# Pair products of both heads in one matmul of 128 rows, on queries copied apart by ScalarE

## The chip, the core and the metric

The kernel runs on one of the eight cores of a Trainium2 chip. A core has five engines with queues of their own: TensorE (PE in the profile; PEld is its weight loads), VectorE (DVE), ScalarE (ACT), GpSimd (POOL) and SyncE (SP), which here issues DMAs. Matrix products go from SBUF, the working memory, to PSUM, eight banks of accumulators. The metric is device time in microseconds (us) of one execution, smaller is better.

## The reference

Two layers of an RWKV block with adaptive layer norms around them, then a feed-forward part with 4-bit quantised operands; 2 batches, 4096 rows, 256 channels, four heads of 64 channels. What the change touches is the recurrence of each head:

```python
def step(state, inp):
    rt, kt, vt, wt = inp
    kv = kt[..., :, None] * vt[..., None, :]
    out = jnp.einsum('bhk,bhkv->bhv', rt, state + u[None, :, :, None] * kv)
    return (state * wt[..., None] + kv, out)
```

The output at row t is the query r_t against the state before it, plus a bonus u for the row's own key and value. The state decays by w, channel by channel, at every row.

## The kernel before

Each batch and layer is walked in 16 blocks of 256 rows: 64 blocks in all. In a block, channels lie on the 128 partitions, in two channel blocks j (two heads each: partitions 0 to 63 and 64 to 127), and the 256 rows are two chunks c of 128. `wkv` (L845) turns the recurrence into matrix products. Within a chunk the weight of the pair (query row t, key row s) is a product of decays between s and t; it is formed level by level. At level l rows are grouped in runs of 2^(l+1); the second half of a run holds queries, the first half keys, and each level multiplies the running products of decay into queries and keys (a DVE product, `pair_view`, L811 and L899) for the level above. `rk` holds queries and keys of a block; `rk2` is a second copy, so that a level can be read while the next is made. Where the copy changes, ACT carries over the half that does not change (L898). Level 0 takes rows in pairs, with the bonus u multiplied in by ACT (`with_bonus`, L818).

`products(l)` (L868) makes the pair products of level l on PE, into the PSUM tile `pa` (two banks). For levels 0 to 4 it goes over two chunks, two channel blocks, four groups q of 32 rows, and the two heads p: 32 matmuls of 64 rows (one head's channels) by 32 columns (the keys of the group), with 32 queries at level 0 and the 16 that are queries at levels 1 to 4 (`queries`, L828). Head p writes bank p. Level 5 has 16 such matmuls, level 6 has 8 of 64 by 64. The products are issued as 0 and 1, 2 and 3, 4 and 5, and 6, each time before the DVE product that overwrites what they read (L887 to L900). DVE then writes each level's pairs through a mask into `diag` (levels 0 to 4, L916), ACT copies levels 5 and 6 and then `diag` into the full 128 by 128 weights `attn` (L919, L928), and `attn` goes against the values v on PE (L961). `kv` are the products of keys and values for the state S.

The order of all work is made by a list planner while the program is built (`Plan`, L118). Nine generators (two batches by two layers, the feed-forward, its two chunks of the last blocks, its weights, the modulation) yield work; each engine's instructions are put out in the order in which the planner expects them to be able to start, from a table of costs (`weight`, L422) and of latencies. Matmuls that follow each other in one generator's step are one piece of work and are not parted. A change of the matmul's shape (rows, columns) counts as a turn of the array. `head_lock` (L696) lets one block at a time into `wkv`, from its bonus to its last product with v. Working tiles come from a stock of 37 slots; a generator goes on only while enough are free (L348). Every recorded instruction has line L294, where the planner gives it out, so tiles' names tell the groups apart.

Of the kernel before, what the change touches and what calls it, by code (L numbers as in the profile page):

```python
# [10 lines left out]
F32 = mybir.dt.float32  # L11
# [7 lines left out]
P = 128  # L19
D = 256  # L20
J = D // P
TT = 256
# [13 lines left out]
SOON = 40.0  # L36
BACK = 104.0
TURNS = 30.0
SLOTS = 37
STAGGER = (12, 60)  # L40
PLANS, JITTER = 1, 8.0
SLOTS2 = 3
# [379 lines left out]
def weight(eng, fn, out, ins):  # L422


    def psum(v):
        return isinstance(v, Later) or v.name.startswith(("pa", "kv"))

    n = max(v.free_size() for v in [out] + ins)
    if eng == "tensor":
        n, rows, cols = out.free_size(), ins[0].shape[0], out.shape[0]  # L430
        if fn == "transpose":
            return 110.0, False
        if rows == P and cols == P:
            return max(4 * n / 2.4 + 6, 195.0 if n == 64 else 265.0 if n == P else 0.0), False
        if n <= 64:
            return {(64, 32): 18.0, (64, 64): 65.0, (P, 64): 65.0}.get((rows, cols), 2 * n), False
        return 0.57 * (4 * n / 2.4 + 6), False
    if eng == "sync":
        return 100.0, False
    wide = [v for v in ins if v.free_size() > 1]  # L440
    if eng == "scalar":
        return 180.0 + n / 1.2 + (85.0 if len(wide) < len(ins) else 0.0), False
    if eng == "gpsimd":
        if out.free_size() <= 8:
            return 360.0 + 170.0 * n, False
        return 90.0 + 2.1 * n, True
    two = sum(not psum(v) for v in wide) >= 2
    if fn in ("tensor_scalar", "tensor_copy"):
        two = not any(psum(v) for v in wide)
        if out.dtype == I32:  # L450
            return 145.0 + n / 1.92, two
    if fn in ("bn_stats", "bn_aggr", "tensor_reduce", "reciprocal"):
        two = False
    if fn == "reciprocal":
        return 150.0 + 6.2 * n, False
    return (205.0 if fn == "scalar_tensor_tensor" and n <= 256 else 150.0) + n / 0.96, two
# [3 lines left out]
def rwkv_adaln_fp4_kernel(ctx: ExitStack, tc: tile.TileContext, a: dict, out: bass.AP):  # L460
# [210 lines left out]
            for m in range(2):  # L671
                nc.gpsimd.memset(carry[i][b][m], 0.0)
    rk2 = keep.tile([P, 2 * J * TT], F32, name="rk2")
    diag = keep.tile([P, 2, C, J, 32], F32, name="diag")
    attn = keep.tile([P, 2, C, J, P], F32, name="attn")
    nc.gpsimd.memset(diag, 0.0)
    nc.vector.memset(kv, 0.0)
    nc.gpsimd.memset(attn, 0.0)
# [136 lines left out]
            v.tensor, v.offset, [v.ap[0], [J * TT - h if changed else J * TT + h, 2], [2 * h, n], [1, h]]  # L815
        )

    def with_bonus(dst, src, odd, u):  # L818

        dv = dst.rearrange("p c j (t two) -> p c j t two", two=2)  # L820
        sv = src.rearrange("p c j (t two) -> p c j t two", two=2)
        pl.scalar.copy(dv[:, :, :, :, 1 - odd], sv[:, :, :, :, 1 - odd])
        for j in range(J):
            pl.scalar.activation(
                dv[:, :, j, :, odd], sv[:, :, j, :, odd], AF.Copy, scale=u[:, j : j + 1]
            )

    def queries(v, l):  # L828
# [7 lines left out]
        t = t[(slice(None),) * len(v.shape) + (1, slice(None))]  # L836
        return t[(slice(None),) * (len(v.shape) - 1) + (0, slice(None))] if l == NLEV - 1 else t

    def level_cols(l):

        wide = [C * J * (64 if m == 6 else 16 if 0 < m < NLEV else 32) for m in range(7)]
        at = sum(wide[0 if l < 4 else 4 : l])
        return slice(at, at + wide[l])

    def wkv(i, b, rk_s, dec_s, v_s):  # L845

# [5 lines left out]
        pl.cur.late = late - RUSH  # L852


        r0, k0 = parts(rk2)
        r, k = parts(rk)
        with_bonus(r0, r, 0, lay[i]["time_first"])
        with_bonus(k0, k, 1, lay[i]["time_first"])
        yield


# [5 lines left out]

        def products(l):  # L868
            R, K = parts(place[l])
            wid = 64 if l == 6 else 32  # L870
            pv = pa[:, :, level_cols(l)].rearrange("p a (c j t) -> p a c j t", c=C, j=J)

            if l < NLEV:
                at0 = [(q, q) for q in (0, 32, 64, 96)]
            else:
                at0 = [(0, 32), (64, 96)] if l == 5 else [(0, 64)]
            for c in range(C):
                for j in range(J):
                    for s0, t0 in at0:
                        for p in range(2):  # L880
                            hp = slice(p * HS, (p + 1) * HS)
                            mm(
                                pv[s0 : s0 + wid, p, c, j, :], K[hp, c, j, s0 : s0 + wid],
                                queries(R[hp, c, j, t0 : t0 + wid], l), True, True,
                            )

        for l in range(7):  # L887
            h = 1 << l
            for m in {1: (0, 1), 3: (2, 3), 5: (4, 5), 6: (6,)}.get(l, ()):
                products(m)  # L890

            n = C * J * P // (2 * h)
            tv = tot.rearrange("p (n two) -> p n two", two=2)
            here, there = place[l] if l else rk, place[l + 1]
            if here is not there:
                pl.scalar.copy(pair_view(there, h, n, False), pair_view(here, h, n, False))  # L898
            pl.vector.tensor_tensor(  # L899
                pair_view(there, h, n), pair_view(here, h, n), tv.rearrange("p n m -> p m n").unsqueeze(3).to_broadcast([P, 2, n, h]), ALU.mult  # L900
            )
            nt = tots_s[:, at : at + n]
            at += n
            pl.vector.tensor_tensor(nt, tv[:, :, 0], tv[:, :, 1], ALU.mult)
            tot = nt

            ready = {3: range(0, 4), 6: range(4, 7)}.get(l, ())
            for m in ready:
                mw = 64 if m == 6 else 32
                mc = level_cols(m)  # L910
                if m < NLEV:
                    dst = queries(diag.rearrange("p a c j t -> p (a c j) t"), m)
                    src = pa[:, :, mc]
                    mask = masks[:, m, : src.shape[2] // (C * J)]
                    mask = mask.unsqueeze(1).unsqueeze(1).to_broadcast([P, 2, C * J, mask.shape[1]])
                    pl.vector.copy_predicated(dst, mask, src)  # L916
                else:
                    for s0, t0 in [(0, 32), (64, 96)] if m == 5 else [(0, 64)]:
                        pl.scalar.copy(  # L919
                            attn[s0 : s0 + mw].rearrange("p a c j t -> p a (c j) t")[:, :, :, t0 : t0 + mw],  # L920
                            pa[s0 : s0 + mw, :, mc].rearrange("p a (n t) -> p a n t", t=mw),
                        )
            yield
        give(dec_s)
# [2 lines left out]
        for q in range(4):  # L927
            qs = slice(32 * q, 32 * (q + 1))  # L928
            pl.scalar.copy(
                attn[qs].rearrange("p a c j t -> p (a c j) t")[:, :, qs],  # L930
                diag[qs].rearrange("p a c j t -> p (a c j) t"),
            )
        bk, pt = pl.bank()
        for c in range(C):
# [21 lines left out]
        for c in range(C):  # L956
            for j in range(J):
                mm(po[:, c, j * P : (j + 1) * P], r[:, c, j, :], S[:, j, :], True, False)
                for p in range(2):
                    hd = slice((2 * j + p) * HS, (2 * j + p + 1) * HS)  # L960
                    mm(po[:, c, hd], attn[:, p, c, j, :], v[:, c, hd], False, p == 1)  # L961
            for j in range(J):
                pl.vector.scalar_tensor_tensor(
                    S[:, j, :], S[:, j, :], tot[:, c, j : j + 1], kv[:, c, j, :], ALU.mult, ALU.add
# [508 lines left out]
```

## Time and profile before

| | |
|---|---|
| median of 3 runs | 3093.93 us (3090.12 to 3097.47) |
| profiled execution: its own time, from first to last instruction (span) | 3081.1 us |
| median less the span | 12.8 us |
| PE busy | 2920.0 us (95%) |
| PEld, weight loads | 2388.7 us (78%) |
| DVE busy | 2345.6 us (76%) |
| ACT busy | 1667.6 us (54%) |
| POOL busy | 1015.7 us (33%) |
| PE records of the pair products (`pa`) | 23552, 278.8 us |
| granted PE clock, mean | 0.981 |

No other time of the profiled execution is given than its span. An fp32 matmul shows as two records on PE and two weight loads. A record's duration holds the way through the array, and records overlap; the pace of a run of equal records is its length less one duration, over the records less one. Idle time in a group's row stands with what ended it. The notation 64*32 in a row is the part of the array that a matmul uses, rows by columns; several such parts work at once where their rows or columns differ. In the last 110 us only the feed-forward of the last blocks is left.

### The profile page before, as it was taken

Reading aid. Unit: us, or ns where it says so; the run is one execution under the profiler, and the core shown is the slowest. Engines: PE = TensorE matmul, PEld = TensorE weight load, DVE = VectorE, ACT = ScalarE, POOL = GpSimd, SP = SyncE. Lnnn points to the kernel's source line nnn. Section 1 sums busy time; section 2 is a strip of 40 time slices with the busy share of each in tenths; the row PEclk is TensorE's granted clock in tenths of the full one; section 3 lists DMA queues with packets and bytes.
Section 4 is the critical chain, followed back from the end, with each engine's and each line's share of the span. In section 5 each row is a group of like instructions: output and inputs, shape, how many; then the busy total and the mean of one; then the engine's idle time right before and its main releaser. Section 6 shows DMA issues by size and latency. Waiting matters only on the chain. (4 is left out here: it accounts for less than half of the span.)

```text
span 3081.1 us, 89987 instructions
## 1 busy us (share of the span) xinstructions
PE 2920.0 (95%) x38460; PEld 2388.7 (78%) x38460; DVE 2345.6 (76%) x6146; ACT 1667.6 (54%) x3478; POOL 1015.7 (33%) x1208
## 2 busy tenths in 40 slices
PE   6899999999999999999999999999999989999997
PEld 4678788777788887888778787787878778787775
DVE  6687876877787877878587777777778776777777
ACT  3465655564565656555564645646456454645452
POOL 2343333333333342333334233242323323232320
PEclk8899999999999999999999999999999999999999
DMA  4000000000000000000000000000000000000000
GB/s 141 12 19 9 15 7 16 3 16 7 13 12 4 20 3 13 11 8 15 5 18 4 10 13 4 19 5 19 4 8 15 3 20 3 6 11 9 9 14 11
DMA packets 35728, 42.56 MB, mean 14 GB/s; under 512 B 2816, under 2 KB 33536, under 8 KB 35328
## 3 DMA queue, kind: packets, MB, share of 16 engines
q1 hardware_dynamic: 35328, 36.81, 3.7%
q8 instruction: 302, 4.95, 0.6%
q14 instruction: 98, 0.80, 0.1%
HBM read 28.41 MB, written 8.39 MB: 12 GB/s over the span
## 5 line engine op out<-in xcount | busy, mean ns | idle before, releaser
L294 POOL TENSOR_TENSOR slot<-slot,slot 128x256 f32<-128x256 f32 (+1 forms) x768 | 578.1, 780 | 819.1 <-DVE slot L294 615.2
L294 ACT ACTIVATE slot<-bank 128x512 f32<-128x512 f32 (+2 forms) x644 | 334.3, 521 | 594.5 <-PE bank L294 563.4
L294 POOL TENSOR_TENSOR tiny<-tiny,nhalf 128x2 f32<-128x2 f32 (+1 forms) x288 | 296.9, 1034 | 874.6 <-DVE tiny L294 852.3
L294 PE MATMUL bank<-slot,cWk 128*128 128x256 f32 x1536 | 364.3, 385 | 4.5 <-DVE slot L294 4.5
L294 PE MATMUL bank<-slot,small 32*128 32x256 f32 (+3 forms) x2816 | 354.9, 359 | 10.3 <-DVE slot L294 6.9
L294 PE MATMUL bank<-cWv,slot 128*128 128x256 f32 x1536 | 342.4, 379 | 0.0
L294 PEld LDWEIGHTS bank<-slot,cWk 128*128 128x128 f32 x1536 | 288.1, 192 | 50.4 <-DVE slot L294 6.5
L294 ACT ACTIVATE slot<-bank,small 128x256 f32<-128x256 f32 (+1 forms) x640 | 250.9, 453 | 138.8 <-PE bank L294 128.7
L294 PEld LDWEIGHTS bank<-cWv,slot 128*128 128x128 f32 x1536 | 290.5, 190 | 39.7 <-issue 0.3
L294 PEld LDWEIGHTS bank<-slot,small 32*128 32x128 f32 (+3 forms) x2816 | 248.5, 178 | 86.2 <-issue 33.9
L294 DVE TENSOR_TENSOR slot<-slot,bank 128x512 f32<-128x512 f32 x192 | 130.7, 681 | 227.2 <-PE bank L294 193.5
L294 DVE TENSOR_TENSOR slot<-slot,slot 128x512 f32<-128x512 f32 x320 | 229.2, 718 | 82.2 <-PE pa L294 46.1
L294 DVE SCALAR_TENSOR_TENSOR slot<-bank,small,slot 128x256 f32<-128x256 f32 x640 | 265.1, 474 | 16.3 <-PE bank L294 16.0
L294 POOL TENSOR_TENSOR slot<-slot 128x512 f32<-128x512 f32 x128 | 140.3, 1098 | 358.4 <-ACT slot L294 253.5
L294 PEld LDWEIGHTS pa<-slot 64*32 64x32 f32 x11264 | 143.5, 109 | 79.9 <-DVE diag L294 35.2
L294 PE MATMUL pa<-slot 64*32 64x16 f32 x11264 | 171.6, 193 | 33.9 <-DVE diag L294 18.8
L294 PE MATMUL bank<-ident,slot 128*128 128x128 f32 x1152 | 176.1, 280 | 22.3 <-DVE slot L294 14.1
L294 DVE SCALAR_TENSOR_TENSOR slot<-slot,small,slot 128x256 f32<-128x256 f32 x384 | 183.4, 516 | 14.9 <-POOL slot L294 14.8
L294 ACT ACTIVATE slot<-slot 128x512 f32<-128x512 f32 x288 | 182.4, 636 | 21.9 <-DVE slot L294 17.3
L294 ACT ACTIVATE slot<-slot,tiny 128x256 f32<-128x256 f32 x256 | 141.6, 596 | 93.3 <-DVE tiny L294 89.9
L294 PE MATMUL bank<-wd,long 128*128 128x256 f32 x768 | 183.0, 389 | 2.2 <-ACT long L294 2.2
L294 PEld LDWEIGHTS bank<-ident,slot 128*128 128x128 f32 x1152 | 136.0, 143 | 57.8 <-DVE slot L294 19.6
(110 smaller groups left out, 5718.7 us busy)
## 6 DMA issues: line engine op xcount, KB each, us to landing
slot<-in_L_attn_x_dram SPq DMA_DIRECT2D x64, 256.0 KB, 2.8
out_dram<-slot SPq DMA_DIRECT2D x64, 128.0 KB, 1.7
slot<-in_L_wmod_dram SPq DMA_DIRECT2D x6, 256.0 KB, 7.7
cWk<-in_L_attn_cWk_dram SPq DMA_DIRECT2D x2, 768.0 KB, 8.1
cWv<-in_L_attn_cWv_dram SPq DMA_DIRECT2D x2, 768.0 KB, 9.4
small<-in_small_dram SPq DMA_DIRECT2D x2, 718.0 KB, 8.4
long<-in_L_ffn_w_down_dram SPq DMA_DIRECT2D x2, 352.0 KB, 2.8
long<-in_L_ffn_w_gate_dram SPq DMA_DIRECT2D x5, 128.0 KB, 2.2
```

Of the source, the lines that this page charges most:

```text
L294: fn(*[real(v) for v in a], **{n: real(v) for n, v in k.items()})
```

## The change

For levels 0 to 4 both heads of a channel block go through one matmul of 128 rows: the keys of 32 rows, all 128 channels, are the weights, and the moving side has two planes, one for each head. In plane p the other head's 64 partitions are zero, so that plane p gives head p's products. The planes lie in three new tiles `own` (level 0; odd levels; even levels), cleared once at the start by POOL; 2048 elements a partition together. Queries are written into the planes by ACT: at level 0 by the bonus, which is issued for each head on its 64 partitions, and at levels 1 to 4 by `apart`, two copies of 64 partitions and 256 elements, issued after the DVE product that makes the level. Levels 0 to 4 then have 16 matmuls each, of 128 rows by 32 columns, with 64 (level 0) or 32 (levels 1 to 4) moving columns. Levels 5 and 6 stay as they are.

The layouts of `diag`, `attn` and `pa` follow: the head is now inside chunk and channel block, and levels 0 to 4 lie each in one bank. The stock has 34 slots for 37. The planner's table has a cost for the new shape.

```diff
@@ -36,7 +36,7 @@
 SOON = 40.0
 BACK = 104.0
 TURNS = 30.0
-SLOTS = 37
+SLOTS = 34
 STAGGER = (12, 60)
 PLANS, JITTER = 1, 8.0
 SLOTS2 = 3
@@ -433,7 +433,7 @@
         if rows == P and cols == P:
             return max(4 * n / 2.4 + 6, 195.0 if n == 64 else 265.0 if n == P else 0.0), False
         if n <= 64:
-            return {(64, 32): 18.0, (64, 64): 65.0, (P, 64): 65.0}.get((rows, cols), 2 * n), False
+            return {(64, 32): 18.0, (P, 32): 17.0 if n <= 32 else 29.0, (64, 64): 65.0, (P, 64): 65.0}.get((rows, cols), 2 * n), False
         return 0.57 * (4 * n / 2.4 + 6), False
     if eng == "sync":
         return 100.0, False
@@ -671,8 +671,11 @@
             for m in range(2):
                 nc.gpsimd.memset(carry[i][b][m], 0.0)
     rk2 = keep.tile([P, 2 * J * TT], F32, name="rk2")
-    diag = keep.tile([P, 2, C, J, 32], F32, name="diag")
-    attn = keep.tile([P, 2, C, J, P], F32, name="attn")
+    diag = keep.tile([P, C, J, 2, 32], F32, name="diag")
+    attn = keep.tile([P, C, J, 2, P], F32, name="attn")
+    own = [keep.tile([P, 2 * J * TT // (1 if m == 0 else 2)], F32, name=f"own{m}") for m in range(3)]
+    for t in own:
+        nc.gpsimd.memset(t, 0.0)
     nc.gpsimd.memset(diag, 0.0)
     nc.vector.memset(kv, 0.0)
     nc.gpsimd.memset(attn, 0.0)
@@ -815,14 +818,16 @@
             v.tensor, v.offset, [v.ap[0], [J * TT - h if changed else J * TT + h, 2], [2 * h, n], [1, h]]
         )
 
-    def with_bonus(dst, src, odd, u):
-
-        dv = dst.rearrange("p c j (t two) -> p c j t two", two=2)
-        sv = src.rearrange("p c j (t two) -> p c j t two", two=2)
-        pl.scalar.copy(dv[:, :, :, :, 1 - odd], sv[:, :, :, :, 1 - odd])
+    def with_bonus(dst, src, odd, u, rows=slice(0, P)):
+
+        dv, sv = (
+            v.rearrange("p c j q (t two) -> p c j q t two", two=2)[rows] for v in (dst, src)
+        )
+        one = "p c j q t -> p (c j q) t"
+        pl.scalar.copy(dv[..., 1 - odd].rearrange(one), sv[..., 1 - odd].rearrange(one))
         for j in range(J):
             pl.scalar.activation(
-                dv[:, :, j, :, odd], sv[:, :, j, :, odd], AF.Copy, scale=u[:, j : j + 1]
+                dv[:, :, j, :, :, odd], sv[:, :, j, :, :, odd], AF.Copy, scale=u[rows, j : j + 1]
             )
 
     def queries(v, l):
@@ -836,11 +841,25 @@
         t = t[(slice(None),) * len(v.shape) + (1, slice(None))]
         return t[(slice(None),) * (len(v.shape) - 1) + (0, slice(None))] if l == NLEV - 1 else t
 
-    def level_cols(l):
-
-        wide = [C * J * (64 if m == 6 else 16 if 0 < m < NLEV else 32) for m in range(7)]
-        at = sum(wide[0 if l < 4 else 4 : l])
-        return slice(at, at + wide[l])
+    def by_head(l):
+
+        return own[0 if l == 0 else 2 - l % 2].rearrange("p (c j q a t) -> p c j q a t", c=C, j=J, q=4, a=2)
+
+    def apart(l, src):
+
+        h = 1 << l
+        sv = src.rearrange("p c j (q n two t) -> p (c j q) n two t", q=4, two=2, t=h)
+        dv = by_head(l).rearrange("p c j q a (n t) -> p (c j q) a n t", t=h)
+        for p in range(2):
+            hp = slice(p * HS, (p + 1) * HS)
+            pl.scalar.copy(dv[hp, :, p], sv[hp, :, :, 1])
+
+    def level_at(l):
+
+        at = {0: (0, 0), 1: (0, 256), 2: (1, 0), 3: (1, 128), 4: (1, 256), 5: (0, 384), 6: (0, 0)}[l]
+        if l < NLEV:
+            return pa[:, at[0], at[1] : at[1] + C * J * (64 if l == 0 else 32)]
+        return pa[:, :, at[1] : at[1] + C * J * (32 if l == 5 else 64)]
 
     def wkv(i, b, rk_s, dec_s, v_s):
 
@@ -852,10 +871,15 @@
         pl.cur.late = late - RUSH
 
 
-        r0, k0 = parts(rk2)
+        _, k0 = parts(rk2)
         r, k = parts(rk)
-        with_bonus(r0, r, 0, lay[i]["time_first"])
-        with_bonus(k0, k, 1, lay[i]["time_first"])
+        by_q = "p c j (q t) -> p c j q t"
+        for p in range(2):
+            with_bonus(
+                by_head(0)[:, :, :, :, p, :], r.rearrange(by_q, q=4), 0, lay[i]["time_first"],
+                slice(p * HS, (p + 1) * HS),
+            )
+        with_bonus(k0.rearrange(by_q, q=4), k.rearrange(by_q, q=4), 1, lay[i]["time_first"])
         yield
 
 
@@ -867,13 +891,20 @@
 
         def products(l):
             R, K = parts(place[l])
-            wid = 64 if l == 6 else 32
-            pv = pa[:, :, level_cols(l)].rearrange("p a (c j t) -> p a c j t", c=C, j=J)
-
+            pv = level_at(l)
             if l < NLEV:
-                at0 = [(q, q) for q in (0, 32, 64, 96)]
-            else:
-                at0 = [(0, 32), (64, 96)] if l == 5 else [(0, 64)]
+                pv = pv.rearrange("p (c j t) -> p c j t", c=C, j=J)
+                for c in range(C):
+                    for j in range(J):
+                        for q in range(4):
+                            qs = slice(32 * q, 32 * (q + 1))
+                            mm(
+                                pv[qs, c, j, :], K[:, c, j, qs],
+                                by_head(l)[:, c, j, q].rearrange("p a t -> p (a t)"), True, True,
+                            )
+                return
+            pv = pv.rearrange("p a (c j t) -> p a c j t", c=C, j=J)
+            wid, at0 = (32, [(0, 32), (64, 96)]) if l == 5 else (64, [(0, 64)])
             for c in range(C):
                 for j in range(J):
                     for s0, t0 in at0:
@@ -881,7 +912,7 @@
                             hp = slice(p * HS, (p + 1) * HS)
                             mm(
                                 pv[s0 : s0 + wid, p, c, j, :], K[hp, c, j, s0 : s0 + wid],
-                                queries(R[hp, c, j, t0 : t0 + wid], l), True, True,
+                                R[hp, c, j, t0 : t0 + wid], True, True,
                             )
 
         for l in range(7):
@@ -903,22 +934,23 @@
             at += n
             pl.vector.tensor_tensor(nt, tv[:, :, 0], tv[:, :, 1], ALU.mult)
             tot = nt
+            if l + 1 < NLEV:
+                apart(l + 1, next(parts(there)))
 
             ready = {3: range(0, 4), 6: range(4, 7)}.get(l, ())
             for m in ready:
                 mw = 64 if m == 6 else 32
-                mc = level_cols(m)
+                src = level_at(m)
                 if m < NLEV:
-                    dst = queries(diag.rearrange("p a c j t -> p (a c j) t"), m)
-                    src = pa[:, :, mc]
-                    mask = masks[:, m, : src.shape[2] // (C * J)]
-                    mask = mask.unsqueeze(1).unsqueeze(1).to_broadcast([P, 2, C * J, mask.shape[1]])
+                    dst = queries(diag.rearrange("p c j a t -> p (c j a) t"), m)
+                    mask = masks[:, m, : 32 if m == 0 else 16]
+                    mask = mask.unsqueeze(1).to_broadcast([P, 2 * C * J, mask.shape[1]])
                     pl.vector.copy_predicated(dst, mask, src)
                 else:
                     for s0, t0 in [(0, 32), (64, 96)] if m == 5 else [(0, 64)]:
                         pl.scalar.copy(
-                            attn[s0 : s0 + mw].rearrange("p a c j t -> p a (c j) t")[:, :, :, t0 : t0 + mw],
-                            pa[s0 : s0 + mw, :, mc].rearrange("p a (n t) -> p a n t", t=mw),
+                            attn[s0 : s0 + mw].rearrange("p c j a t -> p a (c j) t")[:, :, :, t0 : t0 + mw],
+                            src[s0 : s0 + mw].rearrange("p a (n t) -> p a n t", t=mw),
                         )
             yield
         give(dec_s)
@@ -927,8 +959,8 @@
         for q in range(4):
             qs = slice(32 * q, 32 * (q + 1))
             pl.scalar.copy(
-                attn[qs].rearrange("p a c j t -> p (a c j) t")[:, :, qs],
-                diag[qs].rearrange("p a c j t -> p (a c j) t"),
+                attn[qs].rearrange("p c j a t -> p (c j a) t")[:, :, qs],
+                diag[qs].rearrange("p c j a t -> p (c j a) t"),
             )
         bk, pt = pl.bank()
         for c in range(C):
@@ -958,7 +990,7 @@
                 mm(po[:, c, j * P : (j + 1) * P], r[:, c, j, :], S[:, j, :], True, False)
                 for p in range(2):
                     hd = slice((2 * j + p) * HS, (2 * j + p + 1) * HS)
-                    mm(po[:, c, hd], attn[:, p, c, j, :], v[:, c, hd], False, p == 1)
+                    mm(po[:, c, hd], attn[:, c, j, p, :], v[:, c, hd], False, p == 1)
             for j in range(J):
                 pl.vector.scalar_tensor_tensor(
                     S[:, j, :], S[:, j, :], tot[:, c, j : j + 1], kv[:, c, j, :], ALU.mult, ALU.add
```

## The prediction

> **What bounds the kernel now.** I read the page's totals first, then the table of 500 us stretches, then the shapes on TensorE, then what TensorE waits for, and last a timeline of a few blocks for the pace of single matmuls.
>
> ```profile
> span 3081.1 us, 89987 instructions
> ...
> PE 2920.0 (95%) x38460; PEld 2388.7 (78%) x38460; DVE 2345.6 (76%) x6146; ACT 1667.6 (54%) x3478; POOL 1015.7 (33%) x1208
> ```
>
> TensorE (PE) is the only engine near its span. The stretches show that this is not an average over unlike stages:
>
> ```profile
> 0.00:100.00 100.00, 65.54 (x986) 44.65 (x986) 68.76 (x200) 36.58 (x82) 25.26 (x52) 0.88 0.34 114
> 100.00:500.00 400.00, 381.14 (x5245) 315.34 (x5244) 301.60 (x837) 232.49 (x486) 147.15 (x174) 0.97 0.04 12
> 1000.00:1500.00 500.00, 493.61 (x6398) 407.17 (x6396) 387.27 (x1024) 285.99 (x596) 171.40 (x199) 1.00 0.04 11
> 1500.00:2000.00 500.00, 479.09 (x6864) 394.71 (x6852) 380.40 (x1011) 284.11 (x591) 175.21 (x202) 0.98 0.04 11
> 2970.00:3081.10 111.10, 92.82 (x393) 71.26 (x391) 86.42 (x186) 34.49 (x65) 16.81 (x19) 0.95 0.04 12
> ```
>
> The columns after the length are busy us of PE, weight loads, DVE, ACT, POOL, then the granted clock. From 100 to 2850 us PE idles 99.8 of 2750 us in all, so a microsecond of PE work taken out there is nearly a microsecond of time, if the rest keeps up. What PE waits for in that stretch:
>
> ```profile
> PE bank L294 <- DVE slot L294: 19.4, 26, 2.0
> PE pa L294 <- DVE diag L294: 18.5, 24, 1.9
> PE bank L294 <- ACT slot L294: 15.2, 18, 2.4
> ...
> PE kv L294 <- ACT slot L294: 6.9, 12, 1.4
> ...
> PE pa L294 <- ACT attn L294: 3.9, 6, 1.5
> ...
> PE pa L294 <- ACT rk L294: 3.5, 6, 0.9
> ```
>
> ScalarE (ACT) ends only 30.5 us of it (these four ACT lines and 1.0 us for another). The shapes that the change touches, of the pair products (pa) and of the bonus copies:
>
> ```profile
> L294 PE MATMUL pa<-rk 64*32 64x16 f32 x8192 | 96.5, 188 | 8.4 <-DVE diag L294 5.3 <-issue 2.7
> L294 PE MATMUL pa<-slot 64*32 64x16 f32 x8192 | 95.8, 188 | 21.9 <-DVE diag L294 9.4 <-DVE slot L294 6.4 <-DVE tiny L294 4.2
> L294 ACT ACTIVATE rk<-slot,small 128x128 f32<-128x128 f32 x256 | 99.3, 415 | 11.6 <-DVE slot L294 10.6
> L294 ACT COPY rk<-slot 128x256 f32<-128x256 f32 x128 | 54.9, 431 | 0.8
> L294 ACT COPY attn<-diag 32x256 f32<-32x256 f32 x256 | 102.8, 402 | 13.3 <-DVE diag L294 10.3
> ```
>
> Each matmul of this fp32 kernel is two records here. The timeline has the pace (start, length of the run, records):
>
> ```profile
> 1504.45 0.66 PE L294 MATMUL bank<-slot,small 128*64 128x128 f32 x8
> 1505.04 0.73 PE L294 MATMUL pa<-slot 64*32 64x16 f32 x64
> ...
> 1513.01 0.68 PE L294 MATMUL pa<-slot 64*64 64x64 f32 x16 [0.56 <-DVE diag L294]
> 1513.62 0.71 PE L294 MATMUL bank<-slot,small 64*128 64x128 f32 x8
> ...
> 1544.38 0.46 PE L294 MATMUL pa<-slot 64*32 64x32 f32 x32
> ...
> 1556.84 0.69 PE L294 MATMUL kv<-slot,slot 128*64 128x64 f32 x16
> ```
>
> A run's length less one record's mean duration, over the records less one, is the pace. The 64x16 products: (0.73-0.188)/63 = 8.6 ns. Level 5 (N 32, four array tiles at once: two row halves, two column groups; mean 196 ns in its group): (0.46-0.196)/31 = 8.5. Level 6 (64*64, two tiles, N 64, mean 227): (0.68-0.227)/15 = 30.2. kv (128*64, two tiles, N 64, mean 232): (0.69-0.232)/15 = 30.5. The decay projection (128*64, two tiles, N 128, mean 287): (0.66-0.287)/7 = 53.3.
>
> **The change, part by part.** There are 64 blocks (16 row blocks, 2 batches, 2 layers).
>
> Pair products, removed: five levels of 32 matmuls, 320 records x 8.6 = 2.75 us a block. N of 16 or 32 makes no difference to that pace, and neither does having four or eight tiles: it is a floor per record.
>
> Pair products, added: five levels of 16 matmuls, 160 records. Levels 1 to 4 have N 32 on four column tiles. Nearest row: level 5, with the same N, weight columns and number of tiles; only the rows are 128 for 64, and 64*64 against 128*64 (30.2 and 30.5, two tiles each) says that rows alone cost nothing. Low end 8.5, high end half of kv's pace for half its columns, 15.3; I take 8.6, level 5's side. Level 0 has N 64 on four tiles: low end 53.3 x 64/128 x 2/4 = 13.3, high end kv's 30.5 for twice the tiles, 15.3; I take 15. Sum 128 x 8.6 + 32 x 15 = 1.58 us. Saved: 1.17 us a block, 75 us in all (79 at the low ends; 304 ns a block, 19.5 us, if all 160 records go at 15.3).
>
> [...]
>
> Tile shapes: in the built order of instructions the shape changes 968 times before and 1019 times after (mostly 128*32 to 64*32 between levels 4 and 5). One change: level 6's 16 records at 30.2 are 0.48 us, but the next shape starts 0.61 us after (1513.01 to 1513.62), so 0.13 us. +6.5 us; bounds 0 and 6.5.
>
> ACT: the query bonus becomes six instructions on 64 partitions instead of three on 128, and levels 1 to 4 get two copies each. The built program has 576 more copies and 128 more activations, 9 and 2 a block. A 64-partition copy of 256 elements lies between the 402 of 32 partitions and the 431 of 128, so 0.42: 9 x 0.42 + 2 x 0.415 = 4.6 us a block, 295 us. Two more table loads (1283 ns each) are 2.6. ACT goes to 1965 us, 64%: it lies beside PE, but the copies stand before the products. Each copy pair waits for DVE's product of the level before; behind it on ACT's queue wait bank evacuations and the attn copies; PE's products wait for it, and DVE's in-place product of the next level waits for both. Levels 0 and 1, 2 and 3, 4 and 5 stand back to back on PE as before. The cover is other streams' matmuls: between group 0/1 and group 2/3 the built order has, at the paces above, 3.6 us of other PE work (2.7 before), between 2/3 and 4/5 3.0 (3.1), before level 6 1.5 (1.9). Two pairs of copies are 2 x 0.84, inside that. Cost bounds: 0, and all three groups of all blocks waiting a whole pair, 64 x 3 x 0.84 = 161 us. I take the side of the cover, and let ACT's own 30.5 us grow as queues do, by busy/(1-busy): 0.54 gives 1.17, 0.64 gives 1.78, x1.5: +15 us.
>
> Where there is no cover: the first block (PE 65.5 of the first 100 us) and the last two, which the chain of waits runs through from 2926 to 2960 us. Bonus 1.25 us longer and two pairs, 1.7: 3 x 3 = +9 us; bounds 0 and 9.
>
> DVE: the masked copies move as many elements as before; 0, between -2 and +2 us (their 111 us by 2%). POOL clears three tiles once, 2048 elements a partition; diag's 256 took 316 ns, so about 2.5 us under the 34 us that PE idles in the first 100; 0. No DMA is added or moved past another. SBUF: three slots fewer (34 for 37). The least stock for taking on work is unchanged and the cover counted above has not shrunk; I take 0, with an upper bound of the idle growing as 37/34, 9% of 99.8, 9 us.
>
> Sum: -75 + 6.5 + 15 + 9 = -44.5 us on the profiled execution's 3081.1 us span, or 3036.6. The span lies 12.8 us under the median of the runs, 3093.93; I carry that over: **3049.4 us**.
>
> **Rivals.**
> - *The wait takes the place* (slower). ACT serves the copies late, behind evacuations, and the three product groups of each block stand. For it: PE already waits 40 us for inputs of pa in the middle, and the kernel holds one block in this section at a time. Against it: the counted cover, and ACT 36% idle. At the full price: -75 + 6.5 + 9 + 161, 3195 us. It decides from an average of 0.31 us more waiting a group ((75 - 6.5 - 9)/192).
> - *128-row weight loads set the pace.* All records at 15.3: -19.5 + 6.5 + 15 + 9 = +11, 3105 us. For it: kv's pace, the only one with all rows and few columns. Against: 64*64 has the same.
> - *The saving turns to idle time.* The recurrence and DVE's 76% set the time, PE only fills. For it: 4.2% idle from 1500 to 2000 with five streams at work. Against: 1.3% idle from 1000 to 1500, where DVE is as busy. 3094 us, give or take 6.
>
> That the change does not do what it says is out: the built program has 5120 fewer matmuls.
>
> **How the numbers follow.** Forecast 0.77, wait 0.11, pace 0.07, idle 0.05. The likeliest case's own range: all low ends without a stall, -79, 3015; up to 40 us of stalls in place of 15 and ten more for the clock (granted at 0.97 to 1.00 between 100 and 2000 us above), 3085. To leave out no more than 2 in 10 I take 3015 to 3100: under it and beyond it about one in ten each. Under 0.2% (6 us) the measurement can't tell from no change. Faster 0.80 (the forecast and the mild ends of the rivals), same 0.05, slower 0.15.
>
> **What the profile after would show.** Pa records 64*32 fall from 22528 to 2048, and 10240 of 128*32 come; runs of 32 records last about 0.46 us, level 0's about 0.7. PE busy falls by about 70 us, ACT rises to about 1960. If pa waits named for ACT (own, the new tile) add up to over 60 us on PE, the first rival holds; if 128*32 runs last over 0.65 us, the second; if neither and the time stands, the third. The prediction would be wrong on the side of too little if PE's idle time does not grow at all.

## The result and the profile after

The changed kernel takes 3173.97 us (median), the kernel before 3092.56 beside it: 1.0257 times as long, 95% interval 1.0237 to 1.0277. The forecast was 3049.4 us, the range 3015 to 3100. The change made the kernel slower by 81 us.

The page's totals of the changed kernel:

```profile
span 3163.2 us, 70402 instructions
...
PE 2921.9 (92%) x28220; PEld 2365.6 (75%) x28220; DVE 2355.2 (74%) x6146; ACT 1947.6 (62%) x4184; POOL 1021.6 (32%) x1211
```

PE has 10240 records fewer, and is as busy as before (2920.0). The groups by shape, for the products and for ACT's writes into the planes:

```profile
L294 PE MATMUL pa<-own,rk 128*32 128x32 f32 x4096 | 63.6, 206 | 37.3 <-ACT own L294 19.9 <-DVE diag L294 13.4 <-DVE tiny L294 2.0
L294 PE MATMUL pa<-own,slot 128*32 128x32 f32 x4096 | 61.5, 202 | 30.8 <-ACT own L294 13.6 <-DVE diag L294 4.8 <-DVE tiny L294 3.9
...
L294 PE MATMUL pa<-own,rk 128*32 128x64 f32 x2048 | 43.1, 225 | 1.9 <-ACT rk L294 1.9
...
L294 ACT COPY own<-slot 64x256 f32<-64x256 f32 x384 | 159.8, 416 | 38.2 <-DVE slot L294 33.9
...
L294 ACT COPY own<-rk 64x256 f32<-64x256 f32 x256 | 103.1, 403 | 56.5 <-DVE rk L294 49.7 <-DVE slot L294 1.6 <-DVE tiny L294 1.2
...
L294 ACT ACTIVATE own<-slot,small 64x128 f32<-64x128 f32 x256 | 98.5, 408 | 2.2
```

The matmuls themselves are as fast as forecast. The idle time before those of levels 1 to 4 has grown from 30.3 us (8.4 and 21.9 in the rows of before) to 68.1, and ACT's planes (own) end half of it. The same stretches as before, columns as there:

```profile
100.00:500.00 400.00, 371.58 (x3641) 305.34 (x3638) 295.88 (x811) 259.67 (x561) 143.19 (x173) 0.96 0.04 11
...
1000.00:1500.00 500.00, 466.62 (x4694) 381.67 (x4693) 363.67 (x947) 313.00 (x678) 163.26 (x191) 0.96 0.03 10
1500.00:2000.00 500.00, 476.96 (x4516) 388.29 (x4515) 378.57 (x991) 313.47 (x677) 169.41 (x195) 0.97 0.03 9
```

Two things moved. From 1000 to 1500 us PE was idle for 6.4 us before and is for 33.4 now. And the granted clock fell: 0.96 for 1.00 there, 0.961 for 0.981 over the whole run. What PE waits for from 100 to 2930 us:

```profile
PE pa L294 <- DVE diag L294: 34.0, 25, 2.8
PE pa L294 <- ACT own L294: 30.5, 41, 1.9
PE bank L294 <- ACT slot L294: 30.3, 46, 2.1
PE bank L294 <- DVE slot L294: 18.5, 26, 2.4
...
PE kv L294 <- ACT slot L294: 7.4, 13, 1.3
...
PE pa L294 <- ACT attn L294: 4.5, 6, 1.5
```

The planes are one new line of 30.5 us, the evacuations by ACT have doubled (15.2 to 30.3), and the wait put down to the masked copies has grown from 18.5 to 34.0. Over the whole span the lines of ACT sum to 97 us (41 before), those of DVE to 117.5 (91.5).

**Where 82 us of span come from.** At half clock the same run of matmuls takes about twice as long (3.62 us for 1.89, shown below), so I count span x (1 - clock) of PE's busy time as lost to the clock; the rest is work. Before: 2920.0 busy less 3081.1 x 0.019 = 59 leaves 2861 us of work at full clock, and 161 us are idle. After: 2921.9 less 3163.2 x 0.039 = 123 leaves 2799, and 241 are idle. So **work -62, idle +80, clock +64**. The split can be trusted: over the nine kernels with the old products below, work comes out at 2856 to 2862 us, whatever their span, and over the seven with all products of levels 0 to 4 new at 2793 to 2807. But it counts all time at half clock as lost, also where PE was idle in it: 17 of 120 us before, 35 of 251 us after, by the traces' clock records. Counted over PE's busy time alone, work is 2868 to 2876 us in the nine and 2813 to 2818 in the seven, and before to after is work -54, idle +80, clock +56. The table below keeps the first count.

Idle time and clock hang together. This is one block of the changed kernel, PE's timeline:

```profile
1540.55 0.49 PE L294 MATMUL pa<-own,rk 128*32 128x32 f32 x32
1540.97 1.99 PE L294 MATMUL bank<-slot,small 128*128 128x256 f32 x8
1544.89 0.46 PE L294 MATMUL pa<-own,rk 128*32 128x32 f32 x32 [1.93 <-ACT own L294]
...
1549.14 3.62 PE L294 MATMUL bank<-slot,cWk 128*128 128x256 f32 x8
```

PE stands 1.93 us for the planes of level 4. The stretches around it:

```profile
1536.00:1540.90 4.90, 4.54 (x78) 2.82 (x76) 4.74 (x16) 4.43 (x11) 1.48 (x2) 1.00 0.01 3
1540.90:1545.50 4.60, 2.52 (x56) 1.81 (x42) 4.51 (x13) 3.60 (x8) 1.43 (x2) 1.00 0.00 0
1545.50:1552.40 6.90, 6.86 (x68) 5.24 (x69) 6.39 (x17) 3.40 (x8) 2.54 (x5) 0.51 0.01 2
```

In 4.6 us PE was busy for 2.5, at full clock; in the next 6.9 us it was busy throughout, at half clock. A run of 8 records of cWk that takes 1.89 us elsewhere takes 3.62 there. This stall is paid twice.

What did ACT do meanwhile? Its timeline has the pace of its copies:

```profile
1539.64 0.81 ACT L294 COPY own<-rk 64x256 f32<-64x256 f32 x2
1540.48 0.47 ACT L294 ACTIVATE slot<-bank,small 128x256 f32<-128x256 f32 x1
1540.97 1.28 ACT L294 ACT_TABLE_LOAD   x1
1542.27 0.82 ACT L294 ACTIVATE long<-bank 128x352 f32<-128x352 f32 x2
1544.02 0.82 ACT L294 COPY own<-rk 64x256 f32<-64x256 f32 x2 [0.94 <-DVE rk L294]
```

Two copies of 0.403 us take 0.81: the second starts only when the first has ended. Two instructions on all partitions overlap: the pair of 0.463 (128x352) takes 0.82. Over the whole trace of the changed kernel, of pairs that follow each other at once, 1471 on all 128 partitions overlap by 103 ns (median). Pairs on 64 partitions fall into two groups: 158 overlap by 97 ns, and 399 have a gap of 12 ns (11 to 13 for eight in ten). The trace does not name the partitions, but the program does: the two copies into the planes of one level are on different halves, and none of the 127 pairs of own<-slot copies in a row, nor of the 127 of own<-rk, overlaps. The planner's table has every ACT instruction followed 100 ns before its end (`LAP`, L133), so where a copy is followed by one on the other half, ACT is held 0.11 us longer than the order was made for. A copy from slot also takes 23 ns more than its booked cost (416 for 393).

### The profile page after: what moved, and what is told of

Same layout as the page of the kernel before. It is cut to its first block, busy times and chain, and to the rows that moved or that the text cites. A ratio compares the mean times of both kernels' runs of the same rounds, so it can differ in the third digit from the quotient of the medians.

```text
span 3163.2 us, 70402 instructions
## 1 busy us (share of the span) xinstructions
PE 2921.9 (92%) x28220; PEld 2365.6 (75%) x28220; DVE 2355.2 (74%) x6146; ACT 1947.6 (62%) x4184; POOL 1021.6 (32%) x1211
## 5 line engine op out<-in xcount | busy, mean ns | idle before, releaser
L294 PE MATMUL bank<-slot,small 32*128 32x256 f32 (+3 forms) x2816 | 370.4, 365 | 13.8 <-ACT slot L294 8.8
L294 PE MATMUL bank<-slot,cWk 128*128 128x256 f32 x1536 | 373.8, 391 | 2.8 <-DVE slot L294 2.8
L294 PEld LDWEIGHTS bank<-slot,small 32*128 32x128 f32 (+3 forms) x2816 | 255.0, 181 | 93.5 <-issue 34.2
L294 PE MATMUL bank<-ident,slot 128*128 128x128 f32 x1152 | 183.9, 287 | 36.7 <-ACT slot L294 22.2
L294 PE MATMUL bank<-wd,long 128*128 128x256 f32 x768 | 190.0, 399 | 3.0 <-DVE slot L294 1.7
L294 DVE TENSOR_TENSOR long<-long,bank 128x352 f32<-128x352 f32 x256 | 131.3, 515 | 73.6 <-ACT long L294 58.0
L294 ACT COPY own<-slot 64x256 f32<-64x256 f32 x384 | 159.8, 416 | 38.2 <-DVE slot L294 33.9
```

The source lines that it names most:

```text
L294: fn(*[real(v) for v in a], **{n: real(v) for n, v in k.items()})
```

## The experiments

The theories that the expectations name: A, the products wait for ACT's planes, and stalls bring half clock; B, the three slots fewer; C, ACT's load as such makes the evacuations late; D, the longer bonus at the head of each block; E, the order that the planner happens to find; F, the planner books ACT too short, so that its orders are too tight. "Hybrid" is the changed kernel with level 0 left as it was; "booking corrected" is a planner that books ACT longer (the section on theory F has the edit).

Twenty kernels stand beside each other in this table, before and after among them. Idle is span less PE busy; clock loss is span x (1 - clock), work is PE busy less that. All are of one profiled execution, and the clock of one and the same kernel differs between executions (0.974 to 0.981 for the kernel before, which is 20 us of clock loss); the first column is the median of the runs. "Seed" is the draw of the planner's small random ranks; the kernels shown have seed 0.

| kernel | median us | idle | clock loss | work |
|---|---|---|---|---|
| before | 3093 | 161 | 59 | 2861 |
| before, seed 1 | 3124 | 178 | 84 | 2861 |
| before, seed 2 | 3152 | 208 | 85 | 2856 |
| before, 34 slots | 3118 | 178 | 78 | 2860 |
| before, 34 slots, loose copies | 3205 | 230 | 115 | 2858 |
| before, bonus in six | 3174 | 203 | 108 | 2857 |
| before, bonus in six, seed 1 | 3157 | 196 | 95 | 2862 |
| before, booking corrected | 3115 | 174 | 78 | 2856 |
| before, booking corrected, seed 1 | 3116 | 172 | 81 | 2858 |
| after | 3174 | 241 | 123 | 2799 |
| after, seed 1 | 3184 | 262 | 124 | 2799 |
| after, seed 2 | 3195 | 257 | 147 | 2795 |
| after, no copies of levels 1 to 4 | 3095 | 210 | 87 | 2796 |
| after, one head's copies on DVE | 3159 | 240 | 123 | 2796 |
| after, booking corrected | 3129 | 215 | 119 | 2793 |
| after, booking corrected, seed 1 | 3093 | 203 | 84 | 2807 |
| hybrid, level 0 old | 3062 | 171 | 67 | 2823 |
| hybrid, seed 1 | 3123 | 214 | 97 | 2817 |
| hybrid, seed 2 | 3156 | 232 | 123 | 2807 |
| hybrid, booking corrected | 3090 | 184 | 99 | 2803 |

### Is it the slots, ACT's load, or the copies that PE waits for?

Fewer slots alone:

```diff
-SLOTS = 37
+SLOTS = 34
```

> The kernel before with 34 working slots for 37 and nothing else changed. Theory A (the ACT copies stand between DVE's product and PE's products, PE waits, and stretches with much waiting are granted half the clock): 3093 to 3115 us, PE idle time under 30 us more than before. Rival B (three slots fewer leave the planner too little other work to fill in): 3140 us or more, most of the 81 us. Rival C (ACT's load as such delays the bank evacuations): 3093 to 3105 us.

3117.71 us, 1.0078 (1.0061 to 1.0095): 25 us, idle +17. Above the 9 us that the prediction allowed, but far from 81, so rival B's 3140 us is missed. (The seeds below show that 25 us is also what another draw of the order gives.)

The load without the wait:

```diff
-SLOTS = 37
+SLOTS = 34
...
+    dump = keep.tile([P, 512], F32, name="dump")
...
             tot = nt
+            if l + 1 < NLEV:
+                for p in range(2):
+                    hp = slice(p * HS, (p + 1) * HS)
+                    pl.scalar.copy(dump[hp, 256 * p : 256 * (p + 1)], v_s[hp, :256])
```

> The kernel before with 34 slots and eight loose ACT copies of 64 partitions by 256 elements a block, at the same places of the program as in the changed kernel, but from v into a tile that nobody reads: the load without the wait. Theory A: within 25 us of the 34-slot kernel. Rival B: no difference to the 34-slot kernel. Rival C: 50 us or more above the 34-slot kernel, with PE waits for evacuations (PE bank <- ACT) twice as long.

3205.34 us, 1.0362 (1.0341 to 1.0384): 88 us over the 34-slot kernel, where theory A had within 25. Nobody waits for these copies:

```profile
L294 ACT COPY dump<-slot 64x256 f32<-64x256 f32 x512 | 206.5, 403 | 11.6
```

They cost 88 us for 206 us of ACT, in the one draw of the order that was run. So a wait of the products for the planes is not needed for a loss of this size. But rival C was not right in its detail either. PE's waits over the whole span:

```profile
PE pa L294 <- DVE diag L294: 46.5, 42, 3.6
PE bank L294 <- DVE slot L294: 45.4, 40, 12.7
PE bank L294 <- DVE long L294: 36.0, 15, 9.0
PE bank L294 <- ACT slot L294: 23.4, 29, 4.1
```

PE's waits for the evacuations by ACT have not grown: 23.4 us, for 31.6 in the 34-slot kernel. It is DVE's lines that have, 153 us in all for 94 there. DVE itself waits longer for ACT, 305 us over the span for 266, so ACT's lateness may reach PE in part through DVE; the waits alone do not prove that.

The changed kernel without the copies:

```diff
-            if l + 1 < NLEV:
-                apart(l + 1, next(parts(there)))
```

> The changed kernel without the copies of levels 1 to 4; the planes of these levels stay zero, so the pair products of levels 1 to 4 are left out of the result. Matmuls, slots and the bonus by head stay. Theory A: 3020 to 3070 us, time at half clock back from 250 us to under 150. Rival B: 3130 us or more, since the slots are still 34. Rival C: 3040 to 3090 us (same direction as A; the load run tells these two apart).

3094.73 us, 1.0007 (0.9997 to 1.0016). The copies are worth 79 us, but all three forecasts are missed: without the copies the kernel should have been faster than before by some 60 us and is not. Idle is still 210 us, and half clock holds for 173 us, where theory A had under 150. In this draw something beside the copies costs about 50, and what is left in this kernel is the slots and the bonus by head.

### The bonus

Level 0 as before, levels 1 to 4 new, the hybrid (the layouts of own and pa follow; level 0's mask goes over two banks again):

```diff
-SLOTS = 34
+SLOTS = 35
...
-        _, k0 = parts(rk2)
+        r0, k0 = parts(rk2)
...
-        for p in range(2):
-            with_bonus(
-                by_head(0)[:, :, :, :, p, :], r.rearrange(by_q, q=4), 0, lay[i]["time_first"],
-                slice(p * HS, (p + 1) * HS),
-            )
+        with_bonus(r0.rearrange(by_q, q=4), r.rearrange(by_q, q=4), 0, lay[i]["time_first"])
...
-            if l < NLEV:
+            if 0 < l < NLEV:
...
```

> The changed kernel with level 0 as it was before (bonus in three ACT instructions on all partitions, 32 matmuls of 64 rows), levels 1 to 4 in the new form; 35 slots, since a tile of planes is gone. If the eight copies make the loss: 3130 to 3165 us. If the three more bonus instructions at the head of each block make it (PE cannot start level 0 and DVE cannot overwrite the queries before they are done): under 3100 us. If it is the slots: 3150 us.

3062.05 us, 0.99 (0.9884 to 0.9916): faster than both kernels. All eight copies are in it; only three ACT instructions a block, one slot and level 0's matmuls tell it from the changed kernel, and it is 112 us faster.

The bonus alone, in the kernel before:

```diff
...
-        with_bonus(r0, r, 0, lay[i]["time_first"])
+        for p in range(2):
+            with_bonus(r0, r, 0, lay[i]["time_first"], slice(p * HS, (p + 1) * HS))
```

> The kernel before with only the query bonus of level 0 issued for each head (six ACT instructions on 64 partitions for three on 128), into the place where it went before; 37 slots. Theory D (the longer bonus at the head of each block is what hurts): 3130 to 3150 us, since the run without the copies of levels 1 to 4 leaves some 50 us for it. Theory A (the copies and their wait): under 3110 us. If neither the bonus nor the copies cost much alone but both do together: 3095 to 3115 us.

3174.37 us, 1.026 (1.0233 to 1.0286): theory D named 3130 to 3150 and was passed. Three instructions of 0.41 us, 64 times, are 79 us of ACT, and the kernel is 79 us slower, though ACT is idle 45% of the time. That sum looked too round, and every difference so far is of one draw of the order.

### How much is the order that the planner happens to find?

The same kernels with other draws of the planner's ranks: the same work in another order. Only ACT's table loads differ, since the order itself brings them (115, 121 and 125 in the kernel before, 117, 139 and 131 in the changed one, 1.28 us each).

```diff
-    best = min(range(PLANS), key=lambda seed: plan(seed, True))
+    best = min(range(1, 1 + PLANS), key=lambda seed: plan(seed, True))
```

> The kernel before, with the planner's small random ranks drawn from another seed: the same work in another order. Theory E (a good part of the differences is the order that the planner happens to find, not the change): more than 15 us from 3093, either way. If orders are about equally good: 3085 to 3105 us.

> The changed kernel, ranks drawn from the same other seed. Theory E: more than 15 us from 3174. The loss is the change's own if this stays over 3130 us and over the kernel before with this seed by 50 us or more.

> The kernel with level 0 as before and levels 1 to 4 new, ranks drawn from the same other seed. If its gain is its own: under 3085 us, and under the kernel before with this seed. Theory E: more than 15 us from 3062.

> The kernel before with a third seed of the planner's ranks. If the order that was shown is a good draw for this kernel: over 3105 us, as the second seed (3124) and the corrected planner (3115). If 3093 is usual: 3085 to 3100 us.

> The changed kernel with the third seed. If the change costs 60 to 80 us of its own with this planner: 3165 us or more. If half of the loss is the draw: 3125 to 3160 us.

> The kernel with level 0 as before and levels 1 to 4 new, third seed. If levels 1 to 4 alone gain or cost nothing on average: 3060 to 3125 us and no more than the kernel before with this seed. If they cost too: over the kernel before with this seed by 20 us or more.

> The kernel before with the bonus in six instructions, second seed. Theory D (three more ACT instructions at the head of each block cost 50 us or more): 3170 us or more, 50 over the kernel before with this seed (3124). If the 79 us of the first seed are mostly the draw: 3110 to 3150 us.

| seed | before | after | after less before | hybrid less before | bonus in six less before |
|---|---|---|---|---|---|
| 0 | 3093 | 3174 | +81 | -31 | +79 |
| 1 | 3124 | 3184 | +61 | -1 | +33 |
| 2 | 3152 | 3195 | +43 | +4 | not run |

The kernel before spreads over 59 us, and the order that was shown is the best of its three. So part of the 81 us is that a good draw was given up: the three differences have a mean of 62. (A seed does not give two programs the same order, so the rows are not pairs.) The rest comes with the change under this planner: the fastest draw of the changed kernel, 3174, lies above the slowest of the kernel before, 3152. The hybrid's gain is not its own: the new form of levels 1 to 4 is worth 31, 1 and -4 us, so that its 38 to 49 us less work on PE (2823 for 2861, 2817 for 2861, 2807 for 2856) and its copies come out about even. What is lost is lost with the bonus by head: hybrid to after, 112, 61 and 40 us. The bonus in six instructions, second seed, lands at 3157 us, between its two forecasts; the hybrid's third seed, 3156, lies over the 3060 to 3125 forecast for it.

### Is it that the planner books ACT too short?

Only the planner is told something: an instruction on part of the partitions is not overlapped by a next one on others, and costs 25 ns more. The work is the same.

```diff
...
+        if eng == "scalar":
+            v = outs[0].probe if isinstance(outs[0], Later) else outs[0]
+            op.rows = (v.start_partition(), v.shape[0])
+            op.cost += 25.0 if op.rows[1] < P else 0.0
...
         t = max(self.free[op.eng], op.ready)
+        if op.eng == "scalar" and self.rows and self.rows[1] < P and self.rows != op.rows:
+            t = max(t, self.free["scalar"] + self.LAP["scalar"] + 12.0)
...
+        if op.eng == "scalar":
+            self.rows = op.rows
```

> The changed kernel, same work, with the planner told that an ACT instruction on part of the partitions is not overlapped by a next one on other partitions (the traces show 12 ns between them, where two on the same partitions overlap by some 100), and that a 64-partition copy takes 25 ns more than it had. Theory F (the planner books ACT too short, so orders are too tight, PE stands and its clock halves): under 3130 us, with time at half clock under 200 us. If only the load counts, whatever the order: 3150 to 3190 us.

> The kernel before with the same correction of the planner. Its only instructions on part of the partitions are 7 copies a block into attn. Theory F: a little faster or the same, 3070 to 3095 us. If the order found is chance: up to 30 us either way, as another seed gave +28.

> The kernel with level 0 as before and levels 1 to 4 new (35 slots), with the same correction. Theory F: under 3062 us, at best some 3040. If the order found is chance: 3060 to 3125 us, between its two seeds or so.

> The changed kernel with the corrected planner, second seed. Theory F (the planner's booking of ACT makes most of the loss): 20 us or more under the changed kernel with this seed (3184). If the corrected planner's 3129 was a good draw: 3170 us or more.

> The kernel before with the corrected planner, second seed. Theory F: the changed kernel with corrected planner and this seed is no more than 30 us over this one (61 over it without the correction). Its own time: 3100 to 3140 us, as the three draws 3093, 3124 and 3152.

| seed | before, booking corrected | after, booking corrected | after less before | without the correction |
|---|---|---|---|---|
| 0 | 3115 | 3129 | +13 | +81 |
| 1 | 3116 | 3093 | -23 | +61 |

The changed kernel gains 45 and 91 us by the correction, the kernel before -23 and 8. With two seeds each, the gap of 81 and 61 us is gone; the 44.5 us of gain that the prediction summed has not come either (+13 and -23). Theory F holds for the gap, as far as two draws can tell. It did not for each number: with seed 0 the clock loss hardly fell (123 to 119, with 239 us at half clock where under 200 was forecast), the kernel before was to gain a little and lost 23, and the hybrid was to fall under 3062 and rose to 3090, where its other seeds lie around 3123 and 3156. The changed kernel with seed 1, from its page and the totals of its clock:

```profile
span 3093.9 us, 70342 instructions
...
PE 2890.7 (93%) x28220; PEld 2336.6 (76%) x28220; DVE 2356.2 (76%) x6146; ACT 1932.3 (62%) x4192; POOL 1017.0 (33%) x1211
```

```profile
core 0: 3093.9 us, clock 0.973
```

ACT is nearly as loaded as in the changed kernel with this seed (1932 for 1969 us), every product waits for the same planes, and it takes 91 us less: idle 203 for 262, clock loss 84 for 124, work 8 more. PE's waits named for the planes even grow, from 16.3 to 28.9 us. So neither the load nor the chain as such costs the 91 us, but the order in which they were put.

What in the new order helps is not parted. The correction also changes which instructions stand side by side: pairs on 64 partitions that overlap go from 158 to 302 with seed 0 and from 148 to 313 with seed 1, those with a gap from 399 to 278 and from 396 to 280. About 120 such gaps fewer, at 0.11 us, are 13 us of ACT. And it is cautious rather than exact: it denies the overlap also from 64 partitions to all 128, where 96 of 261 such pairs in the changed kernel overlap, by 94 ns.

### Shorter chain

```diff
-            pl.scalar.copy(dv[hp, :, p], sv[hp, :, :, 1])
+            (pl.scalar.copy if p else pl.vector.tensor_copy)(dv[hp, :, p], sv[hp, :, :, 1])
```

> The changed kernel with head 0's copies of levels 1 to 4 on DVE and head 1's on ACT, so that a level waits for one copy and not for two in a row, and ACT has four fewer a block. If the wait for ACT is the cause (theory A): 3110 to 3140 us. If the bonus alone is (theory D): over 3150 us.

3159.19 us, 1.0201 (1.0177 to 1.0224): 15 us under the changed kernel, inside what a draw of the order does; over theory A's 3110 to 3140, and in theory D's, over 3150. DVE has 56 us more to do (2411.6 for 2355.2). Halving the copies that a level waits for on ACT does not bring the time back.

## Why the prediction was wrong

**Right: the pace of the matmuls.** Levels 1 to 4 run at 8.7 ns a record (8.6 taken, 15.3 feared), level 0 at 14.0 (15 taken), the mean from start to start over the trace at full clock. A line for each of them in the changed kernel:

```profile
1534.63 0.65 PE L294 MATMUL pa<-own,rk 128*32 128x64 f32 x32
1535.10 0.48 PE L294 MATMUL pa<-own,slot 128*32 128x32 f32 x32
```

(0.65 - 0.225)/31 = 13.7; the next starts 0.47 us after. So the choice of level 5's pace over half of kv's held: these tiles use all 128 rows, and with weight loads of 115 ns and matmuls of 204 ns a record in the mean, a record still starts every 8.7 ns, so loads and matmuls of this group run beside each other here. The second rival is out. PE's work fell by 54 to 62 us, by the two ways of counting the clock; 68.5 was the sum with the shape changes.

**Right: ACT's load.** 1965 us forecast, 1947.6 measured; the durations of the 64-partition instructions (0.40 to 0.42) were well placed.

**Wrong: "ACT's own 30.5 us grow as queues do: +15 us".** This is the step that failed. PE's idle time grew by 80 us, not by 15 + 9. In size the first rival came: its point was 0.31 us more waiting a group, and 80 us over 192 groups are 0.42. But its mechanism, the products waiting for the planes, is the smaller half, and its sign, over 60 us of PE waits for own, did not come: 30.5 us stand by that name (33.6 over the whole span; PE's weight loads stood 89.0 us for own, but PE was idle for it only those 33.6). The others are evacuations and DVE's results that come late, and loose copies that nobody waits for cost as much.

**Why the cover failed.** The prediction counted 3.6 and 3.0 us of other matmuls between the groups in the built order, and took them for cover. The prediction itself charged a pair of copies its full 0.84 us; but the order in which it counted the cover was made by the planner, whose table has 0.393 for such a copy and lets the next start 0.1 us before its end: 0.69 us for a pair, where the trace after has 0.81. The trace of before already showed otherwise:

```profile
2269.82 1.64 ACT L294 COPY attn<-diag 32x256 f32<-32x256 f32 x4
```

Four attn copies in a row, on four sets of 32 partitions, take 1.64 us for four of 0.402: no overlap, where the planner's table has 0.1 us. Cover in an order that is itself worked out from booked times is no evidence that the times are right. Nine of the eleven new ACT instructions a block are copies, eight of them in pairs on alternating halves. Correcting the booking removes the gap in both seeds tried; that is shown. How the lateness travels from ACT to PE in each block is not: in the changed kernel the waits name DVE more (117.5 us) than ACT (97).

**Wrong: "ten more for the clock".** The clock cost 64 us more (56 over busy time alone). The stretch of 4.6 us quoted above is how: a stall of 1.9 us brings some 7 us at half clock. In the table, kernels with more idle time than before have 0.5 to 2 us of clock loss more for each us of it. The clock records of the twenty traces show the step between: the clock changes only at marks 3.41 us apart. Of the stretches between two marks that ran at full clock, all 301 in which PE was busy for less than 0.4 of the time were followed by half clock, 360 of 1437 with 0.4 to 0.8, and 5 of 15326 with more. The traces of before and after alone have 28 of 28, 35 of 154 and 0 of 1528. So in these traces idle time that gathered in one such stretch came with half clock in what followed, the more often the more of it there was. No run changed the clock by itself.

**Wrong: the slots at 0, 9 at most.** 25 us with seed 0. It is not settled how much of that is the draw. The 12.8 us that the sum carries from span to median is no fixed offset either: in the profiled executions after it, the time lies 1.8 to 2.2 us over the span, so some 11 us of it is probably that the profile of before shows one of the shortest executions (its clock, 0.981, is the highest seen of that kernel).

**Not thought of: the draw.** The built order of a list planner is one of many, and the kernel before stood on a good one. Its other two seeds are 31 and 59 us slower. The range ended at 3100, since I gave the first rival 0.11 and left its price, 3195 us at the full, outside; the result lies inside that price.

What stays open is why the bonus in six instructions costs so much more than its share (79 and 33 us with two seeds, when the eight copies of levels 1 to 4 come out even with what they save). Its place, ahead of everything in a block, suggests that it delays all that follows; no run moved it, and none has it alone with the booking corrected.

## What to carry to other kernels

Work taken off the bounding engine is worth its time only if what replaces it on other engines is booked at the price that the trace shows back to back, not at its mean duration less a usual overlap: read the pace of equal instructions in a row first. Where a program orders itself by a table of costs, run a second draw of the unchanged kernel before crediting or blaming a change: here the draws of one kernel differ by 59 us, more than half of the effect. And look whether a stall of TensorE is paid twice, once as idle time and once as clock: here 80 us of idle came with 56 to 64 us of clock.

## What the runs showed of the hardware

- In the changed kernel, back-to-back ACT instructions on all 128 partitions overlapped by 103 ns (median of 1471 pairs). Copies into the planes, which change from one half of the partitions to the other, did not overlap in any of 254 pairs and had a gap of 12 ns (median); of all 557 pairs on 64 partitions, 399 had a gap, 12 ns in the median. The split by heads paid that in this kernel: 0.81 us for two copies of 0.403.
- Matmuls on 128 rows by 32 columns with four column tiles took 8.7 ns a record at 32 moving columns and 14.0 at 64; 64 rows by 32 columns with 16 or 32 moving columns took 8.5 to 9.0. From 16 to 32 moving columns only the number of records counted here.
- In the changed kernel, half clock followed a stretch in which PE was only partly idle (busy 2.5 of 4.6 us, the longest wait 1.93 us). In these traces a stretch of 3.41 us with PE busy under 0.4 of it was always followed by half clock (301 of 301), one over 0.8 almost never (5 of 15326).
